# One convolution-attention and expert kernel: the norm's power ahead of the diagonals, table rows filled in the first stage, and steps of the convolution and of the experts moved between stages

## The chip, the cores and the metric

The kernel runs on one core of a Trainium2 chip. The metric is the device time of one execution in microseconds (us), as a median over runs. Engines are named as the profile names them: PE (TensorE, matrix products), PEld (its weight loads, which run beside the products), DVE (VectorE), ACT (ScalarE), POOL (GpSimd) and SP (SyncE, which here only issues transfers). ACT and POOL issue transfers too. Each engine runs its own list of instructions in order.

## The reference, cut to what matters

```python
def _gn(v, G=32, eps=1e-5):           # group norm over channels and places
    ...
    return ((g - m) / jnp.sqrt(s + eps)).reshape(v.shape)

# layer 0; x is (2, 256, 56, 56), f32
def _L0_conv_ref(x, w_qkv1, w_qkv2, rpb0, rpb1, w_proj):
    y = jnp.einsum('oc,bchw->bohw', w_qkv1, x)              # 256 -> 768 channels
    y = jax.lax.conv_general_dilated(y, w_qkv2, (1, 1), 'SAME', feature_group_count=3 * C)
    ...                                                     # q, k, v of 8 heads
    outs.append(_natten2d(q[:, sl], k[:, sl], v[:, sl], rpbs[s], 7, DILATIONS[s]))  # 7x7, dilation 1 and 2
    ...
    return jnp.einsum('oc,bchw->bohw', w_proj, o)
x = x + _L0_conv_ref(_gn(x), ...)

# layer 1; tokens t, 3136 for each of two images
    Q = jax.nn.elu(q) + 1.0
    K = jax.nn.elu(k) + 1.0
    KV = jnp.einsum('nshd,nshv->nhdv', K, v)                # sums over all tokens of an image
    msg = jnp.einsum('nlhd,nhdv,nlh->nlhv', Q, KV, Z) * L
    msg = _layernorm(msg.reshape(N, L, C) @ Wm, g1, b1)
    h = jax.nn.relu(jnp.concatenate([x, msg], axis=-1) @ W1) @ W2
t = t + (x + _layernorm(h, g2, b2))
    ...
    probs = jax.nn.softmax(xt @ Wr + br, axis=-1)           # 8 experts, the best 2 for each token
    h = jax.nn.gelu(jnp.einsum('end,edh->enh', xe, W1) + b1[:, None, :], approximate=False)
    y = jnp.einsum('enh,ehd->end', h, W2)
t = t + (weights[:, :, None] * sel).sum(axis=1)
```

## The kernel before, in words

**Stages.** The two images are shifted against each other, so that work of two kinds is there at any time.

1. Start and first stage (0 to 418 us): image 0 is loaded and normed, its convolution runs, and then image 0's neighbourhood attention runs while image 1 is normed and part of its convolution is made. At the end the projection of image 0 is added to the input and written as tokens to `td`.
2. Key sums of half 0, image 0's tokens (460 to 547 us): for each tile of tokens a layer norm, keys and values, and their sums.
3. Groups of half 0 (547 to 780 us): queries, message, feed-forward, router and the scatter of routed tokens into the rows of `xs`.
4. The seam (780 to 860 us) and attention of image 1 (to 1078 us), between whose steps stand the first steps of the experts.
5. Key sums of half 1 (1106 to 1211 us), its groups (1211 to 1476 us) and the router's tail (1476 to 1511 us), with further experts' steps.
6. The last stage (from 1511 us): all other expert tiles, one after the other, and the output.

**Norm and convolution** (class `Convolutions`, L400). An image lies in `x_sb` as two blocks of 128 channels by 3136 places. `load_x` fetches it in two halves of columns, block 0 on SP's queue and block 1 on ACT's. `norm_image` takes statistics in seven columns of G = 448 places (bn_stats on DVE), sums them over a group by a small matrix product, and `rstd_of` takes the power -1/2 on POOL; then DVE norms `x_sb` in place, in two halves. It is a generator: image 1's runs between taps of image 0's last block. `run` makes a qkv block (`oc`, six of them, in two halves `hf`): four products of eight rows into `py` (L510), each copied by ACT into the padded `ypad` (L516), and then nine taps into `yc`. While `share` is in force (the first stage), eight rows of a half go to PE: nine diagonal matrices `diag` are made by POOL (L500) and multiplied (L529), and DVE does the other rows. Without it (the rest of image 1's convolution, run inside layer 1) DVE does all the taps (L549), at a priority lowered by LATE. A store on SP (L564) closes a half of a block. What is left of it in layer 1 are 26 calls of the generator: 24 blocks `py`, one call ahead without PE work, and the last taps.

**Attention** (class `Attention`, L593). Bias tables are loaded by row as `tab0` and `tab1` in the pool `t`, one buffer each; the chunk's scores (L622), bias, Exp, sums and values follow. `residual` (L879) loads the input of two tiles into `x_s` on SP, ordered behind the newest convolution store `anchors["store"]`; `projection` takes it. The pools' letters give the order in which their memory is laid out: t tables, k keys, b bias, p probabilities, v values, r, x and ac for output and sums, l loads.

**Layer 1** (`linear`, L1574, called from `layer1`, L2059). It yields steps: `keys` 39 of them, then `steps` (L2041) takes a list of strings, `parts`, one for each group of tiles plus the drain. Each letter asks one generator for one step:

- q queries, m message, f feed-forward, r and p the router's two ends, P a scatter, w the merging of the sums, x preparation of the router
- k a step of the convolution (half 0 only)
- e a step of the experts (half 1 only); c has no work of its own

In half 0, `fill()` gives the convolution a step at every third step of the key sums. After `parts[7]` a loop empties the generator. Then come `ln.keep()`, the fill of `y2` (L2093, a tile with constants) and seven fills of `xs` (L2096, 256 rows of 260 floats each, the rows that pad short expert lists), and the load of the first experts.

**Experts** (class `Experts`, L1283). Tiles have 256 routed rows. `ex.run` yields two steps ahead and eight per tile; a step is eight products (L1536 into `ph`, or L1554 into `py`), and a finished tile is added to `y2` by an indirect transfer on POOL (L166). NFI = 13 tiles run early: as steps inside attention of image 1 from its step LEAD = 12 on, inside the key sums of half 1 and at the letters e. The other NFS - NFI = 35 full tiles and NHS = 5 half tiles run in the last stage.

**What sets the order.** On PE, layer 1 and attention of image 1 run exactly as written (`tc.manual_schedule`). On the other engines, and on PE in the first stage, a planner orders the instructions: it simulates when operands are there, and prefers what comes earlier in the code, unless `tc.high_priority` shifts it (a negative offset puts it last). `tc.issue_after(ins)` keeps an instruction behind `ins` if both are on the same engine; on another engine it orders nothing:

```python
with tc.issue_after(anchors["store"]):
    ld = nc.sync.dma_start(x_s[:, :, : kn * TT], xv[b, :, :, i * TT : (i + kn) * TT])
```

`anchors["pow"]` is the newest power of a norm (on POOL), `anchors["store"]` the newest store of the convolution (on SP). `rstd_of` is a helper; its lines L149 and L259 appear in the profile.

## Time and profile before

| what | number |
|---|---|
| median of 3 runs | 2087.62 us |
| lowest, highest | 2083.85, 2088.35 us |
| profiled execution, its own time | 2087.87 us |
| its span | 2086.1 us |
| instructions | 27767 |
| bytes moved by DMA, mean rate | 268.78 MB, 129 GB/s |
| L510 on PE (`py`, qkv blocks) | 384, 152.4 us |
| L1536 and L1554 on PE (experts) | 1440 and 1360, 306.9 and 303.7 us |
| L166 on POOL (indirect transfers of experts) | 101, 162.3 us |
| L529 on PE (diagonals) | 324, 132.6 us |

The page of the profile gives for each engine the busy time and its share of the span, the number of instructions behind an x, and the chain of work that ended last. A view by stretch gives the same busy times for a window of the span. A waits' line names the engine that waited, what it then ran, "<-" and the instruction that released it, and behind the colon the total in us, the number of waits and the longest one. In a line of the timeline the first two numbers are start and duration, and a number in square brackets is the time from which the operands were there, with what came last. "SPq" is SP's queue of transfers. PE's clock is the granted clock as a share of full speed. The longest groups of instructions are those of the table; all PE groups together make the 89% busy share.

### The profile page before, as it was taken

How to read it: one execution, taken by the hardware profiler on the slowest of the kernel's cores; microseconds unless marked ns; L12 is line 12 of the kernel's file. 1: busy time of each engine (PE TensorE's matmuls, PEld its weight loads, DVE VectorE, ACT ScalarE, POOL GpSimd, SP SyncE). 2: the span in 40 equal slices, each digit the busy share in tenths (PEclk: the TensorE clock that was granted, in tenths of full speed). 3: DMA queues.
4: the chain of work that ended last, by engine and by line, in shares of the span. 5: the costliest groups of instructions: out<-in, count | busy, mean ns of one | idle time of the engine just before them, and what ended most of it. 6: DMA issues, size and time to landing. Idle time of an engine off the chain costs nothing.

```text
span 2086.1 us, 27767 instructions
## 1 busy us (share of the span) xinstructions
PE 1857.6 (89%) x9996; PEld 1320.8 (63%) x9996; DVE 1071.3 (51%) x2696; ACT 678.2 (33%) x1271; POOL 630.4 (30%) x738
## 2 busy tenths in 40 slices
PE   4999998967889994799988899999599999999996
PEld 2545454545646553566666665567488888888885
DVE  4988988858977654465554333555342111211121
ACT  1333333312334322444433433334122222222332
POOL 4532110037211444111115611234433333333231
PEclk9999899989999996799999999999799999999998
DMA  5542431250101228664475121011387766766895
GB/s 119 138 120 81 135 110 44 79 172 16 39 31 39 69 89 235 146 158 125 113 204 155 49 58 38 31 51 54 97 241 209 201 192 190 199 194 190 281 286 173
DMA packets 198426, 268.78 MB, mean 129 GB/s; under 512 B 30377, under 2 KB 157399, under 8 KB 198033
## 3 DMA queue, kind: packets, MB, share of 16 engines
q1 hardware_dynamic: 173584, 230.43, 36.1%
q0 software_dynamic: 19728, 27.54, 7.2%
q10 hardware_dynamic: 4960, 8.88, 1.2%
q8 instruction: 83, 1.36, 0.3%
q14 instruction: 71, 0.57, 0.1%
HBM read 200.11 MB, written 70.95 MB: 130 GB/s over the span
## 4 chain that ended last, share of the span: by engine, by line
PE 69%; DVE 12%; DMA 7%; POOL 5%; ACT 3%; issue 3%; SPq 0%; ACTq 0%; DVEq 0%; POOLq 0%
PE ph L1536 13%; PE py L1554 12%; PE p L1849 8%; PE pc L529 4%; PE py L510 4%; PE po L636 4%; PE py L1865 4%; PE x L1554 2%; DVE yc L549 2%; PE x L1536 2%; DMA y<-yt,idi 2%; PE pm L1819 2%; PE s_ps L622 2%; DVE yc L556 2%; PE pq L1779 2%
## 5 line engine op out<-in xcount | busy, mean ns | idle before, releaser
L1536 PE MATMUL ph<-xe,w1e 128*128 128x256 f32 (+1 forms) x1440 | 306.9, 370 | 4.0 <-ACT hT L1540 2.2
L1554 PE MATMUL py<-w2e,hT 128*128 128x256 f32 x1360 | 303.7, 380 | 0.0
L1540 ACT ACTIVATE hT<-ph,sv 128x256 f32<-128x256 f32 (+1 forms) x360 | 165.1, 461 | 406.9 <-PE ph L1536 396.5
L1536 PEld LDWEIGHTS ph<-xe,w1e 128*128 128x128 f32 x1440 | 262.8, 191 | 39.4 <-ACT hT L1540 2.5
L1554 PEld LDWEIGHTS py<-w2e,hT 128*128 128x128 f32 x1360 | 255.0, 191 | 33.7 <-issue 1.7
L166 POOL DMA_INDIRECT y<-yt,idi x101 | 162.3, 1607 | 270.3 <-DVE yt L1560 126.7
L556 DVE SCALAR_TENSOR_TENSOR yc<-ypad,w,yc 128x1120 f32<-128x1120 f32 x144 | 199.3, 1385 | 27.9 <-ACT yc L546 25.3
L510 PE MATMUL py<-x_sb,wq 128*128 128x448 f32 (+1 forms) x384 | 152.4, 531 | 12.9 <-DVE x_sb L481 9.6
L259 POOL TENSOR_TENSOR rs<-rs,mhalf 128x2 f32<-128x2 f32 (+3 forms) x90 | 69.2, 773 | 312.3 <-DVE rs L258 231.2
L627 DVE TENSOR_TENSOR p<-p,tab 112x952 f32<-112x952 f32 (+5 forms) x88 | 122.1, 1391 | 61.8 <-ACT p L626 56.3
L626 ACT ACTIVATE p<-s_ps 112x952 f32<-112x952 f32 (+5 forms) x88 | 102.1, 1160 | 138.1 <-PE s_ps L622 92.7
L529 PE MATMUL pc<-ypad,diag 128*128 128x448 f32 x324 | 132.6, 549 | 0.0
L1492 DVE CAST idi<-xr 128x2 int32<-128x2 f32 (+1 forms) x53 | 10.9, 205 | 235.3 <-DMA xr<-xs 235.3
L1560 DVE SCALAR_TENSOR_TENSOR yt<-py,eq,yt 128x256 f32<-128x256 f32 x85 | 41.0, 483 | 164.7 <-PE py L1554 164.7
L1518 POOL TENSOR_SCALAR yt<-b2e,eq 128x256 f32<-128x256 f32 x101 | 48.8, 490 | 242.5 <-DMA b2e<-in_L_ffn_b 180.4
L510 PEld LDWEIGHTS py<-x_sb,wq 128*128 128x128 f32 x384 | 72.2, 197 | 75.5 <-issue 55.8
L166 POOL DMA_INDIRECT xs<-row,si x98 | 96.5, 984 | 70.9 <-DVE si L1985 37.0
L549 DVE SCALAR_TENSOR_TENSOR yc<-ypad,w,yc 128x784 f32<-128x784 f32 x96 | 109.0, 1145 | 7.3 <-ACT yc L546 6.2
L636 PE MATMUL po<-p,v 98*32 98x170 f32 (+5 forms) x960 | 69.9, 370 | 32.9 <-DVE p L627 15.8
L1849 PE MATMUL p<-m2T,fw 128*128 128x512 f32 (+2 forms) x224 | 95.2, 549 | 0.0
L305 PE MATMUL kx<-xt,ks 128*128 128x256 f32 (+1 forms) x200 | 59.1, 446 | 39.7 <-DVE ks L242 39.7
L1849 PE MATMUL p<-xT,fw 128*128 128x512 f32 (+1 forms) x208 | 94.0, 576 | 0.0
(370 smaller groups left out, 2927.0 us busy)
## 6 DMA issues: line engine op xcount, KB each, us to landing
w1e<-in_L_ffn_W SPq DMA_DIRECT2D x53, 1024.0 KB
w2e<-in_L_ffn_W SPq DMA_DIRECT2D x53, 1024.0 KB
yd<-yc SPq DMA_DIRECT2D x24, 784.0 KB
ld<-yd SPq DMA_DIRECT2D x28, 448.0 KB
xr<-xs SPq DMA_DIRECT2D x48, 260.0 KB
b2e<-in_L_ffn_b SPq DMA_DIRECT2D x53, 128.0 KB
t<-td SPq DMA_DIRECT2D x12, 512.0 KB
y<-t SPq DMA_DIRECT2D x24, 256.0 KB
```

Of the source, the lines that this page charges most:

```text
L166: ins = nc.gpsimd.indirect_dma_start(out=dst[:, :], out_offset=bass.IndirectOffsetOnAxis(ap=index, axis=0), in_=src, in_offset=None, **kw,)
L510: nc.tensor.matmul(py[:, :n, :], self.wq1[:, ct, oc * P : (oc + 1) * P], self.x_sb[:, ct, (q0 + g0) * WW : (q0 + g0 + n) * WW], start=(ct ...
L529: nc.tensor.matmul(pc, diag[:, tap, :], ypad[:, dy : dy + SHARE, dx : dx + WW], start=(tap == 0), stop=(tap == 8),)
L549: nc.vector.scalar_tensor_tensor(yc[:, y0:y1, :], src, w, yc[:, y0:y1, :], ALU.mult, ALU.add)
L556: nc.vector.scalar_tensor_tensor(yc[:, y0:y1, :], src, w, yc[:, y0:y1, :], ALU.mult, ALU.add)
L626: nc.scalar.activation(p[:nk, :, :n], s_ps[:nk, :, :n], AF.Exp)
L627: nc.vector.tensor_tensor(grid(p), grid(p), table[:nk], ALU.mult)
L636: nc.tensor.matmul(dst[hs] if w is None else den[hs], v[:nk, hs] if w is None else w[:nk, :], p[:, h, :, o : o + q.shape[2]], start=first ...
L1536: nc.tensor.matmul(p1, x.w1[:, ct, j * P : (j + 1) * P], x.xe[:, ct, :], start=(ct == 0), stop=(ct == 1),)
L1540: nc.scalar.activation(hT[:, j, :], p1, AF.Gelu, bias=x.sv[:, 4 + j : 5 + j])
L1554: nc.tensor.matmul(py, hT[:, j, h * P : (h + 1) * P], x.w2[:, j, :], start=(j == 0), stop=(j == NJ - 1),)
L1849: nc.tensor.matmul(p1[:, :w], fw1[:, k, oc * P : (oc + 1) * P], rhs, start=(k == 0), stop=(k == 3))
```

## The change

It has five parts.

1. **Norm.** `load_x` fetches an image in four pieces of columns (448, 896, 896, 896) instead of two. The power stands under `tc.high_priority()`. The norm is applied in three pieces (448, 1120, 1568 columns) instead of two. The diagonals stand on POOL behind the newest power.
2. **First stage.** The projection at the end of image 0 keeps two residual loads ahead, in three buffers instead of two, and from strip 3 on they are not ordered behind a store. The pools of image 0's attention and of `linear` for half 0 are laid out in another order. For image 1, `tab0` has two buffers.
3. **Fills.** The fill of `y2` and the seven of `xs` stand ahead of layer 1 in the code, under `issue_after(anchors["pow"])`, instead of behind its first eight parts.
4. **Convolution in half 0.** The key sums give it a step at i = 0, 1, 2, 13, 19, 25, 31 and 37 (8 instead of 13), the parts 16 instead of 13: two more strings have a third k and a second, so the k per string are 4, 3, 3, 2, 2, 2 instead of 4, 3, 3, 2, 1, 0. The last two calls are left to the loop after part 7.
5. **Experts.** NFI is 14: one tile more runs early. The key sums of half 1 give 23 steps instead of 15. In the strings of half 1 the letters e move from the middle parts, 6 to 8, towards their ends and to the last parts; some of the other letters there change their order.

```diff
-NFI = 13
+NFI = 14
...
         def load_x(self, b):
-            for hf in range(2):
-                cols = slice(hf * T // 2, (hf + 1) * T // 2)
+            for c0, c1 in zip((0, G, 3 * G, 5 * G), (G, 3 * G, 5 * G, T)):
+                cols = slice(c0, c1)
                 for ct in range(2):
...
-            grs, anchors["pow"] = rstd_of(sp, gps[:, 2:4], 1e-5, "gn")
-            yield
-            for hf in range(2):
-                cols = slice(hf * T // 2, (hf + 1) * T // 2)
+            with tc.high_priority():
+                grs, anchors["pow"] = rstd_of(sp, gps[:, 2:4], 1e-5, "gn")
+            yield
+            for c0, c1 in zip((0, G, T // 2), (G, T // 2, T)):
+                cols = slice(c0, c1)
...
-                        for tap in range(9):
-                            nc.gpsimd.tensor_scalar(
-                                diag[:, tap, :], ident, w2[:, oc, tap : tap + 1], 1.0, ALU.mult, ALU.mult
-                            )
+                        with tc.issue_after(anchors["pow"]):
+                            for tap in range(9):
+                                nc.gpsimd.tensor_scalar(
+                                    diag[:, tap, :], ident, w2[:, oc, tap : tap + 1], 1.0, ALU.mult, ALU.mult
+                                )
...
-                t = self.pool["t"].tile([TT, NH * (KR[s] + 6) * nw], F32, name=f"tab{s}")
+                t = self.pool["t"].tile(
+                    [TT, NH * (KR[s] + 6) * nw], F32, name=f"tab{s}", bufs=2 if self.banks and s == 0 else 1
+                )
...
-                x_s = xp.tile([P, 2, 2 * TT], F32, name="x_s")
+                x_s = xp.tile([P, 2, 2 * TT], F32, name="x_s", bufs=2 if banks else 3)
                 i = e[j] + k0
-                with tc.issue_after(anchors["store"]):
+                with tc.issue_after(anchors["store"]) if banks or j < 3 else nullcontext():
...
-                        acc, items = strip(j)
-                        for _, k0, kn in items:
-                            projection(acc, j, k0, kn, residual(j, k0, kn))
+                        items = [(j, k0, min(2, e[j + 1] - e[j] - k0)) for k0 in range(0, e[j + 1] - e[j], 2)]
+                        loaded = deque(residual(*item) for item in items[:2])
+                        acc, _ = strip(j)
+                        for k, item in enumerate(items):
+                            projection(acc, *item, loaded.popleft())
+                            if k + 2 < len(items):
+                                loaded.append(residual(*items[k + 2]))
                             yield 0
...
-        att = Attention(ctx, 0, "l t k b p v r x ac")
+        att = Attention(ctx, 0, "l k b t p v r x ac")
...
-        pools = {k: pool(f"p3{k}", bufs[k]) for k in ("q e t w k l s", "e s t q k w l")[half].split()}
+        pools = {k: pool(f"p3{k}", bufs[k]) for k in ("e t q w k l s", "e s t q k w l")[half].split()}
...
+        with tc.issue_after(anchors["pow"]) if behind else nullcontext():
+            nc.sync.dma_start(y2[N : N + ST, :], a["c_fill"][0, :, 0:C])
+            for i in range(NDUM):
+                rows_i = slice(E * RG + i * ST, E * RG + (i + 1) * ST)
+                nc.sync.dma_start(xs[rows_i, :], a["c_fill"][E + i])
         with ExitStack() as ph:
             ln = linear(ph, tk, 0, behind)
             with tc.manual_schedule(engines={mybir.EngineType.PE}):
                 for i, _ in enumerate(ln.keys()):
                     if i == 5:
                         ln.feed()
-                    if i % 3 == 1:
+                    if i < 3 or (i > 8 and i % 6 == 1):
                         fill()
...
-                    "mqfkfPPPPmkqfrfrff", "mqfkpPPPPfmqfrfrff", "mqfpPPPPfmqfrfrff",
+                    "mqfkfPPPPmkqfrfrff", "mqfkpPPPPfmkqfrfrff", "mqfkpPPPPfmkqfrfrff",
...
             ln.keep()
-            nc.sync.dma_start(y2[N : N + ST, :], a["c_fill"][0, :, 0:C])
-            for i in range(NDUM):
-                rows_i = slice(E * RG + i * ST, E * RG + (i + 1) * ST)
-                nc.sync.dma_start(xs[rows_i, :], a["c_fill"][E + i])
...
-                    if i < 3 or i % 3 == 1:
+                    if i < 3 or i % 3 == 1 or (i < 27 and i % 3 == 2):
                         next(tiles, None)
...
-                    "qewexewexqwexqq", "meqemeq", "meqefmqfefefff",
+                    "qewexewexqwexqq", "meqemeq", "meqfmqfeffff",
...
-                    "mqfpcfmfqrfPPfPrPfe", "mqfpfmfqePePrePfePref", "mfefpefmeferePPfePerPe",
-                    "fefeepefeferePfePere", "eeeeperPePer", "eeeepP",
+                    "mqfpcfmfqrfPPfPrPf", "mqfpfmfqPPrPfPref", "mffpfmfrePPfPerPe",
+                    "ffepfefreePfePere", "eepeereePeePer", "eeepePe",
```

## The prediction

> **What bounds the kernel now.** I read the page first (engine shares, the chain), then busy time by stretch, then the waits inside each stretch with idle TensorE, then the order of the instructions there. The page says TensorE is the bound: 1857.6 us busy of 2086.1, and the chain is 69% PE. So the work itself stays, and only the 228 us without it can go. This view by stretch (length, then busy us of PE, PEld, DVE, ACT, POOL, then PE clock, DMA share, GB/s) shows where they lie:
>
> ```profile
> PE 1857.6 (89%) x9996; PEld 1320.8 (63%) x9996; DVE 1071.3 (51%) x2696; ACT 678.2 (33%) x1271; POOL 630.4 (30%) x738
> ...
> 0.00:36.00 36.00, 6.69 (x13) 3.39 (x13) 13.13 (x29) 2.03 (x4) 10.09 (x35) 0.99 0.54 137
> 418.00:460.00 42.00, 24.18 (x89) 17.32 (x90) 22.87 (x78) 3.57 (x6) 14.32 (x24) 0.76 0.69 213
> 460.00:547.00 87.00, 70.11 (x292) 52.52 (x291) 76.02 (x119) 28.40 (x48) 58.79 (x53) 0.94 0.05 19
> 620.00:780.00 160.00, 157.36 (x603) 96.06 (x601) 97.70 (x395) 53.31 (x146) 55.20 (x62) 1.00 0.18 59
> 780.00:860.00 80.00, 42.14 (x276) 25.48 (x277) 33.76 (x153) 19.64 (x33) 25.84 (x33) 0.59 0.76 197
> 1106.00:1211.00 105.00, 85.57 (x401) 70.89 (x399) 41.56 (x132) 44.92 (x64) 63.45 (x84) 0.97 0.28 81
> 1476.00:1511.00 35.00, 13.99 (x71) 11.62 (x70) 15.37 (x112) 3.90 (x11) 16.30 (x17) 0.69 0.40 118
> 1511.00:1958.00 447.00, 445.60 (x2120) 392.52 (x2120) 101.11 (x363) 117.42 (x248) 140.58 (x157) 0.99 0.71 202
> ```
>
> The idle places are the start (29 us), the end of image 0 and the first key sums (18 + 17), the seam into image 1 (38), the second key sums (19) and the router's tail (21). From 620 to 780 and from 1511 on TensorE is full; there any work added costs its price. Next the waits of PE in 418 to 547, in 1106 to 1211 and in the tail, and one of SP before the seam (total us, times, longest), then the start in order of time:
>
> ```profile
> PE kx L305 <- DVE ks L242: 23.7, 12, 6.8
> ...
> PE kx L305 <- DVE ks L242: 16.0, 11, 3.7
> ...
> PE pp L1976 <- DVE chosen L1968: 20.6, 3, 9.2
> ...
> SPq L2096 <- DMA xs<-row,si: 16.0, 1, 16.0
> ```
>
> ```profile
> 18.43 6.26 POOL L500 TENSOR_SCALAR diag<-ident,w 128x128 f32<-128x128 f32 x18 [15.95 <-DMA w<-in_L_conv_w_qkv]
> ...
> 25.45 0.72 POOL L149 TENSOR_TENSOR rs_gn<-rs_gn,mhalf 128x2 f32<-128x2 f32 x1
> ...
> 35.25 0.23 ACT L370 ACTIVATE pf<-pf 84x33 f32<-84x33 f32 x1 [31.02 <-DMA pf<-frame]
> ...
> 35.95 5.22 PE L510 MATMUL py<-x_sb,wq 128*128 128x448 f32 x8 [3.12 <-ACT ypad L516]
> ```
>
> **A, the start.** The input of the power is there at 17.96 and the power runs at 25.45, behind 18 diagonals. Moved ahead: 7.5 us earlier. The first norm piece shrinks from 1568 to 448 columns, from 1.03 us (four took 4.12) to about 0.3: 0.7 more. But the gain meets a second wait. ScalarE's queue holds `pf`'s Exp (L370) ahead of the first `ypad` copies, and that Exp waits for a DMA until 35.25; TensorE had two banks full at 32.8 and stood 3.1 us for it. If ScalarE's order stays, TensorE resumes at 35.95 as before: gain 0. If all copies of the first block come ahead of the Exp, two banks are full at 27.36 - 8.2 + 5.5 = 24.6, and the gain is 11.3. The second Exp, at 39.01, stands in the same queue. The order is the planner's, and its times shift by only a few us, so some copies pass and not all: I take -4.5. x in four pieces per row block instead of two puts four more issues of about 0.43 us on the two queues (1.7 us, half on SP ahead of `frame`), so the Exp may come 1 us later. Statistics: the last wave holds 4 of 14 bn_stats instead of 8, 4 x 0.54 = 2.1 us at best; I count it in the -4.5. Upper end: the seven fills below get ahead of the second `pf` load on SP, 1.9 MB at the 231 GB/s of the stretch from 780 to 800 is 8 us: +8.
>
> Against cutting x speaks the Trainium skill, "DMA: Bandwidth & Descriptors", "Anatomy of one DMA": about 2.0 us fixed for each DMA, bytes on top. The row: the second halves (1.61 MB on both queues) were ready at 10.94, 3.8 us after the first at 7.17, which is 426 GB/s with no fixed cost between. By the page, if two more waves each paid it, A would be -0.5; by the row it stays.
>
> The same edit applies to image 1. Its diagonals now queue behind its power at 249.94; they were made at 237.07 in 4.13 us, and their first use is at 266.42, so 250.7 + 4.1, or 11.3 (the longest nine diagonals took), ends before that: free, but without that cover up to 7 us. Two more norm operations on DVE: 0.1 us; the first matmul starts about 0.7 earlier. **B** is this and the end of image 0: residual loads two ahead in three buffers, and from strip 3 not behind a store. The last residual went out at 428.63, `w_k` and the token loads stand behind it on SP, tokens land at 436.14 and PE waits 6.8 us for their norm. With a buffer more it can go after the third item's transposes, about 426.4: -2. The projections themselves wait for the one `s_ps` tile, which stays. The pools' new order lets tokens land where `l` and `k` lay; these are done by 403, as the tables are by 407: nothing before the residual. B together -2.5, from -6 to +2.
>
> **C, key sums to groups.** The convolution has 24 blocks left (L510), about 1.25 us of PE each, and 96 taps (L549) of 1.14 us on DVE, 16 to a chunk of four blocks. Calls needed: 26. Before, 13 in the key sums and 13 in the groups. After, 8 (three at once at the start, where PE waits 6.8 us anyhow) and 16; the last two fall to the loop that empties the generator, after part 7, at the seam. In 460 to 547 the taps are 53.5 of DVE's 76.0 us; one chunk (18.3) is left of them. PE has 70.1 - 7 x 1.25 = 61.4 us there, and of 17 us idle, which wait for `ks` behind taps, I keep 8: 87 - 70 = -17. Given back: five blocks go into a stretch that is full, 5 x 1.25 = +6.3, and 18 us of taps among DVE's 97.7 of 160 cost about 1 us of lateness. C -10; ends: -20 if idle goes altogether and the moved blocks find gaps, +5 if ks stays late for POOL's sake (58.8 of 87 us busy).
>
> **D, the seam, 780 to 860.** Removed: seven fills (1.9 MB, 4.44 us of SP at 776.18, after 16.0 us in which SP stood for scatters). Their bytes sit in front of the loads that end PE's waits: `ld` took 9.28 us to land, `tab` 6.32. Without 8 us of traffic `ld` lands some 5 us sooner. The p of the first chunk, 7.5 us late, has a second cause: `sv` before it on DVE waits for POOL's scatters to 812.7; half gained, say 0 to 7. Two buffers for the first table let its second row load ahead of `w1e` and `w2e`; the wait until 850.32 (6.3 us, table landing) goes. The 8.7 us for `ld` behind 4 MB of weights stays, and is late next. Added: block 24 (1 us PE), 16 taps (18.3 us, DVE has 46 free but queues in order), and eight Experts loads (4 us of SP) that waited for x_sb at 648 and now wait until 779, in front of the tables; the late tap of 1.1 us on some of the router's steps: +4. D = -5 - 3 - 6 + 4 = -10; ends -20 and, with the store below, +15.
>
> Clock: granted 0.59 in that stretch. The skill's "TensorE: Matmul & The Clock Gate", Part 1, says an idle window of about 3.4 us halves it; by that rule, shorter waits would also speed part of the 42.1 busy us, and D could reach -18. I left it out of the sum.
>
> The fills land in the first 100 us instead, DMA share 0.51 there from 36 on; SP issues them in its gaps (4.44 us). The next need of that queue, attention's `ld` at 71.8, feeds PE at about 100: hidden; uncovered, the 8 us of A's upper end.
>
> **E, experts.** Steps of `tiles`: 2 + 8 per tile, 106 before, 114 now. Attention takes 65 in both. Before: 15 in the key sums, 26 in parts 0 to 8; the 21 after that find nothing. Now: 23 in the key sums, 10 in parts 0 to 2, none to part 6, 1, 3, 7, and 5 of 9 in part 10. A step is eight matmuls, 1.75 us. The eight new ones in the key sums stand just where PE waits for `ks` (16.0 us in 11): cost 6 instead of 14, -8. In the tail, twelve steps (21 us) stand among three waits of 7.5, 9.2 and 3.9; by position one step precedes the first, three the second, none the third, and the rest lengthens the chain: they cover about 10. Given back: parts 6 to 8 lose ten steps, waits of 1.8 to 3.6 us such as those at 1421 to 1425 appear: +3; a tile's POOL work (two scatters of 1.6, so 0.4, two yt of 0.49, 4.6 us) stands in the router's queue: +3. E = -12. One tile, 14.25 us from one `ph` to the next, leaves the full last stage and appears here: no sum of its own. Ends -20 and +3.
>
> **Sum** against the profiled execution, 2087.87 us (span 2086.1 and 1.8 around it; median 2087.62): -4.5 - 2.5 - 10 - 10 - 12 = -39: 2049, said as 2050.
>
> **Rivals.** (1) All lower ends: 2088 - 77 = 2011, some of it won't add, 2020; for it: every wait named has another engine idle; against: `sv` and `pf`. (2) Given back: A 0 behind `pf`, C -3 since 620 to 780 is full, D -3, E -5, B -2: 2075. (3) Slower: SP's order puts the last convolution store (L564) ahead of the seam's loads. It must wait for 16 taps that start after 778. In the profile two such stores held SP 78.3 us, the longest 48.2, harmlessly, as nothing was due. At the seam attention's loads are. Held to about 812 (778 + 18.3 + DVE's own 12.7 + copies) it costs 27 and the sum is near zero; 48 gives 2088 - 39 + 10 + 48 = 2107. It decides from 33 us on. Against it: DVE is less than half busy there and the planner ranks taps last. (4) The fills change nothing because SP already floated the y2 fill to 33.55; but the xs fills did stand at 776.
>
> **How the numbers follow.** Likeliest 0.45, its own range 2032 to 2068; given back (2068 to 2083) 0.20; all (under 2032) 0.13; no change 0.05; slower 0.17. Faster 0.78, same 0.05 (within 0.2%, 4.2 us, about what a measurement of this kernel tells from none), slower 0.17. The range 2020 to 2094 leaves out about 0.06 below and 0.13 above.
>
> **What would show it.** Power before the diagonals near 18, and PE's first steady run well before 36, with `pf`'s Exp behind some `ypad` copies (A). First key sums about 17 us shorter, L510 in them seven (C). No xs fill from 776 to 781, PE busy above half from 780 on (D). Waits of `kx` for `ks` in the second key sums halved, experts in the tail, 34 full tiles in the last stage (E). Wrong would be: SP standing in L564 at the seam, a router tail 10 us longer than what its steps take, or the last stage not 14 us shorter.

## The result, and the profile after

The changed kernel took 2102.37 us (median of 3, 2101.07 to 2105.39) against 2087.62: a ratio of 1.0078, interval 1.0053 to 1.0104. It is slower, by 15 us, where 2050 had been forecast. The profiled execution spans 2099.0 us, 12.9 more than that of before.

First the same stretches as before, in the view by stretch (length, then busy us of PE, PEld, DVE, ACT, POOL, then PE clock, DMA share, GB/s), behind the page's line of the engines:

```profile
PE 1868.1 (89%) x9996; PEld 1324.4 (63%) x9996; DVE 1067.6 (51%) x2700; ACT 677.8 (32%) x1271; POOL 636.1 (30%) x738
...
0.00:36.00 36.00, 10.28 (x21) 5.67 (x22) 13.71 (x31) 2.90 (x5) 13.09 (x38) 0.92 0.53 140
418.00:460.00 42.00, 26.25 (x91) 17.46 (x92) 24.98 (x76) 5.59 (x9) 13.61 (x25) 0.80 0.67 208
460.00:547.00 87.00, 65.75 (x271) 50.46 (x270) 54.19 (x108) 20.54 (x37) 51.23 (x55) 0.88 0.02 10
620.00:780.00 160.00, 160.00 (x615) 98.08 (x613) 104.50 (x397) 55.90 (x149) 59.62 (x61) 1.00 0.17 57
780.00:860.00 80.00, 39.03 (x253) 23.57 (x252) 39.34 (x166) 19.12 (x35) 28.07 (x33) 0.59 0.73 188
1106.00:1211.00 105.00, 92.17 (x430) 77.87 (x428) 43.61 (x136) 43.79 (x65) 65.35 (x85) 0.95 0.36 101
1476.00:1511.00 35.00, 26.85 (x132) 22.24 (x130) 12.21 (x69) 10.26 (x21) 15.90 (x17) 0.90 0.32 91
1511.00:1958.00 447.00, 433.64 (x2039) 379.31 (x2040) 106.88 (x412) 116.00 (x241) 140.93 (x156) 0.98 0.68 192
```

Two rows answer the prediction at once. From 460 to 547 DVE lost 22 of its 76.0 us (the prediction's taps come to 35), and PE did not get denser: 65.8 busy instead of 70.1, at a granted clock of 0.88 instead of 0.94, and the stage ends where it ended. From 1511 on PE, full before (445.6 of 447), is no longer: 433.6.

Fixed windows slide when a stage is longer, so the rest is read from landmarks of PE: the first or last product into a tile that only one stage uses. The landmarks of a single profile move by several us, in the first stage above all (the first key product of half 0 lies between 435.4 and 444.9 in fifteen profiles with the new start), so lengths of stages are compared, and means where there are several. The profiles are before and after and those of the runs below.

| stage, from landmark to landmark | old form, us | new form, us | difference |
|---|---|---|---|
| start to first key product `kp` (5 and 15 profiles, means) | 440.1 | 441.6 | +1.5 |
| first `kp` to last `pk`, key sums half 0 | 104.1, 104.2 | 99.7 to 102.7, 7 profiles, mean 101.2 | -2.9 |
| last `pk` to last `p`, groups half 0 | 224.3, 222.9 | 225.2 to 226.0, 7 profiles | +2.3 |
| last `p` to first `po` of image 1, seam | 42.2 to 45.0, 5 profiles, mean 43.6 | 46.4 to 46.7, 11 profiles | +3.0 |
| key sums half 1, with 15 and with 23 expert steps | 103.1, 103.2 (101.0 to 106.0 in 6 profiles) | 113.6 to 115.4, 5 profiles, mean 114.6 | +11.4 |
| last `pk` to last `pp` of half 1, groups and tail | 299.5 (299.2 to 302.4 in 6 profiles) | 304.9 (298.9 to 304.9 in 3 profiles) | +5.4 |
| last `pp` to last `ph`, last stage | 547.1 | 540.0 (540.0 to 543.6 in 3 profiles) | -7.1 |

What the prediction had as -39 us is thus +13: A and B +1.5, C -0.6, D +3.0 (and in the attention behind it +0.8 in the mean, with a scatter of 5 us), E +9.7. The +1.5 and the +5.4 are inside the scatter of their landmarks, the other rows are not. Groups, tail and last stage together are steadier: 846.6 to 850.6 us with the old strings and 13 tiles, 842.5 to 844.9 with the new ones and 14, so the tile that was to take 14.25 us off them took 2 to 8. PE's waits in the first key sums (460 to 547), then in the second (1106 to 1226), then in the tail and the head of the last stage (1476 to 1620):

```profile
PE kx L305 <- DVE ks L242: 21.3, 11, 6.3
...
PE ph L1544 <- ACT hT L1548: 7.0, 5, 2.3
PE kx L305 <- DVE ks L242: 5.3, 4, 1.6
PE pts L275 <- DVE xe L1520: 2.4, 2, 1.2
...
PE pp L1984 <- DVE chosen L1976: 9.6, 2, 5.5
PE ph L1544 <- ACT hT L1548: 6.5, 2, 5.4
PE ph L1544 <- DVE xe L1520: 3.3, 2, 2.2
PE px L1517 <- DMA xr<-xs: 1.8, 1, 1.8
```

Every wait that the experts' steps took away in the second half has an heir: for `ks` 16.0 us became 5.3, but the steps themselves now wait for `hT` and `xe`; in the tail a wait for `hT` of 5.4 us is new; in the last stage, where PE had waited 1.1 us, it waits 5.1 us for an expert tile's rows and what is made of them.

### The profile page after: what moved, and what is told of

Read it like the earlier page. It is cut to its first block, busy times and chain, and to the rows that moved or that the text cites. A ratio compares the mean times of both kernels' runs of the same rounds, so it can differ in the third digit from the quotient of the medians.

```text
span 2099.0 us, 27775 instructions
## 1 busy us (share of the span) xinstructions
PE 1868.1 (89%) x9996; PEld 1324.4 (63%) x9996; DVE 1067.6 (51%) x2700; ACT 677.8 (32%) x1271; POOL 636.1 (30%) x738
## 4 chain that ended last, share of the span: by engine, by line
PE 68%; DVE 11%; DMA 8%; ACT 4%; POOL 4%; issue 4%; SPq 1%; another core or an unknown queue 0%; ACTq 0%; DVEq 0%; POOLq 0%
PE py L1562 12%; PE ph L1544 12%; PE p L1857 7%; PE py L512 5%; PE pc L531 5%; PE po L638 4%; PE py L1873 3%; PE x L1562 3%; PE kx L305 2%; PE x L1544 2%; DVE yc L551 2%; DMA y<-yt,idi 2%; PE s_ps L624 2%; PE pm L1827 2%; PE pq L1787 2%
## 5 line engine op out<-in xcount | busy, mean ns | idle before, releaser
L1544 PE MATMUL ph<-xe,w1e 128*128 128x256 f32 (+1 forms) x1440 | 315.4, 376 | 17.2 <-ACT hT L1548 13.5
L1544 PEld LDWEIGHTS ph<-xe,w1e 128*128 128x128 f32 x1440 | 266.0, 194 | 55.7 <-ACT hT L1548 15.3
L259 POOL TENSOR_TENSOR rs<-rs,mhalf 128x2 f32<-128x2 f32 (+3 forms) x90 | 68.6, 766 | 267.9 <-DVE rs L258 237.9
L1500 DVE CAST idi<-xr 128x2 int32<-128x2 f32 (+1 forms) x53 | 11.4, 215 | 239.9 <-DMA xr<-xs 239.9
L166 POOL DMA_INDIRECT xs<-row,si x98 | 103.3, 1054 | 83.0 <-DVE si L1993 46.0
L551 DVE SCALAR_TENSOR_TENSOR yc<-ypad,w,yc 128x784 f32<-128x784 f32 x96 | 100.7, 1061 | 2.9 <-ACT yc L548 2.1
L531 PEld LDWEIGHTS pc<-ypad,diag 128*128 128x128 f32 x324 | 60.8, 193 | 53.3 <-issue 49.4
```

The lines of the kernel that those rows point to most:

```text
L166: ins = nc.gpsimd.indirect_dma_start(out=dst[:, :], out_offset=bass.IndirectOffsetOnAxis(ap=index, axis=0), in_=src, in_offset=None, **kw,)
L531: nc.tensor.matmul(pc, diag[:, tap, :], ypad[:, dy : dy + SHARE, dx : dx + WW], start=(tap == 0), stop=(tap == 8),)
L551: nc.vector.scalar_tensor_tensor(yc[:, y0:y1, :], src, w, yc[:, y0:y1, :], ALU.mult, ALU.add)
L1544: nc.tensor.matmul(p1, x.w1[:, ct, j * P : (j + 1) * P], x.xe[:, ct, :], start=(ct == 0), stop=(ct == 1),)
```

## The experiments

Ratios are to the kernel before, run beside, with a 95% interval. Three questions came in this order: which part lost the time, why the key sums did not get shorter, what the seam and the last stage wait for.

### Which part lost it

**The experts' part undone.**

```diff
-NFI = 14
+NFI = 13
-                    if i < 3 or i % 3 == 1 or (i < 27 and i % 3 == 2):
+                    if i < 3 or i % 3 == 1:
...
-                    "ffepfefreePfePere", "eepeereePeePer", "eeepePe",
+                    "fefeepefeferePfePere", "eeeeperPePer", "eeeepP",
```

> The changed kernel with the experts' part undone (13 early tiles, 15 steps in the second key sums, the letters e as before). Theory: the experts' part is what made the kernel slower, about 10 of the 13 us between the two spans, since its steps lengthen the router's tail; this run is then at about 2092 us (2088 to 2096). Rival: the loss was there before the experts (start, key sums, seam), and this run stays at 2100 to 2104.

2089.02 us, ratio 0.9997 (0.9981 to 1.0013): no change from before. The theory holds, with two consequences. E costs 13 us by these medians (14 when each is set against its own kernel before), 10 by its stages; and the other four parts together, forecast at -27, are worth nothing.

**The experts' part alone**, on the kernel before (the same edit the other way).

> The kernel before with the experts' part alone. Theory: about 2098 us, 10 more than before, with the second key sums some 10 us longer for 14 us of steps, and the tail from the last full group to the first tile of the last stage some 17 us longer. Rival (the experts' part only loses together with the other parts, which delay it): 2086 to 2090.

2095.46 us, 1.0035 (1.0017 to 1.0052), which is 7 us slower, a little less than expected. The second key sums took 115.4 us instead of 103.1, groups and tail 303.2 instead of 299.5, the last stage 541.5 instead of 547.1. So it loses alone, and the interval leaves it open whether it loses more in company.

**The letters as before, with the tile and the 23 steps kept.**

```diff
-                    "mqfpcfmfqrfPPfPrPf", "mqfpfmfqPPrPfPref", "mffpfmfrePPfPerPe",
-                    "ffepfefreePfePere", "eepeereePeePer", "eeepePe",
+                    "mqfpcfmfqrfPPfPrPfe", "mqfpfmfqePePrePfePref", "mfefpefmeferePPfePerPe",
+                    "fefeepefeferePfePere", "eeeeperPePer", "eeeepP",
```

> The changed kernel with 14 early tiles and 23 steps in the second key sums, but the letters e of the strings as before (26 steps, none left for the last three strings). Theory: the place of the steps in the tail costs the time, not the tile: the tail is then as short as before (33 us from 1478 to 1511), the last stage a tile shorter but for 4 to 7 us of waits, and the whole 2092 to 2095 us. Rival (the tile costs more early than late, wherever it stands): 2100 to 2104.

2095.15 us, 1.0031 (1.0014 to 1.0047). Groups and tail are back at 300.9 us, 4 less than with the new letters; as other profiles of the new letters lie between 298.9 and 304.9, the stage alone does not show it, and what carries the reading are the medians, 2095.15 and 2102.37. The last stage stayed at 542.1, so the tile brings 5 us there, not 14.25.

**The new strings, with 13 tiles.**

```diff
-NFI = 14
+NFI = 13
```

> The changed kernel with 13 early tiles: the strings stay, and the eight steps that are missing leave the last strings empty. Theory: the tail loses eight steps of 1.75 us that lengthened the router's chain and the last stage gains a tile of 14.25 us without its waits; 2090 to 2095 us. Rival (tail and last stage exchange the tile one for one): 2100 to 2104.

2094.68 us, 1.0020 (1.0005 to 1.0035). Eight steps fewer make groups and tail 289.2 us instead of 304.9, 15.7 for 14 us of products: in the sum these steps were not covered at all. They did fill waits (for `chosen` PE waits 18.6 us here and 9.6 with them), but other waits came in their place. The last stage went from 540.0 to 547.5. A tile that costs its full price early saves half of it late.

What the tail's steps do is in ACT's timeline of the changed kernel there (start, length, instruction, and in brackets the idle time before and what ended it):

```profile
1506.46 0.47 ACT L1548 ACTIVATE hT<-ph,sv 128x256 f32<-128x256 f32 x1 [0.39 <-PE ph L1544]
1507.73 0.47 ACT L1548 ACTIVATE hT<-ph,sv 128x256 f32<-128x256 f32 x1 [0.79 <-PE ph L1544]
1508.22 1.28 ACT L1909 ACT_TABLE_LOAD   x1
1512.79 0.22 ACT L1909 ACTIVATE prob<-prob 128x16 f32<-128x16 f32 x1 [3.29 <-DVE prob L1908]
1513.02 1.28 ACT L1548 ACT_TABLE_LOAD   x1
1514.32 0.84 ACT L1548 ACTIVATE hT<-ph,sv 128x256 f32<-128x256 f32 x2
```

```profile
1511.16 0.41 DVE L153 TENSOR_SCALAR row<-t_ab,mv,rs 128x256 f32<-128x256 f32 x1 [3.28 <-DMA xs<-row,si]
```

The experts' Gelu and the router's Exp take turns on ACT, in order. The Exp holds the queue 3.3 us until DVE has its input, and DVE for its part waits 3.28 us for the landing of a scatter (the second view, of DVE). Each change of function loads a table for 1.28 us. Together that is PE's 5.4 us for `hT`. From the last feed-forward product to the end of the router there are four such loads (5.1 us), before there was one. The prediction had looked at PE's gaps in the tail and counted them as cover, not at the queue that the steps need besides PE.

### Why the key sums stayed as long

**No convolution step in the key sums of half 0.**

```diff
-                    if i < 3 or (i > 8 and i % 6 == 1):
+                    if False:
                         fill()
```

> The changed kernel without the experts' part and without any step of the convolution in the key sums of half 0; all eight go to the loop behind part 7, so that the seam is longer and only the key sums are looked at. They take 101 us from the first key product to the last, with eight steps, and 104 in the kernel before with 13. Prediction's theory (the taps on DVE make the sums late): 80 to 88 us. Rival (a chain of its own from one tile to the next sets the pace: key product, two steps of ACT, DVE, sum product, norm of the next tile): 95 to 101 us.

102.9 us. No step at all is no shorter than eight. It is a single run, 2114.73 us in all, as the steps now stand at the seam. The view of this stage, 442 to 544, for this kernel:

```profile
442.00:544.00 102.00, 69.40 (x269) 54.87 (x268) 36.55 (x113) 17.45 (x32) 52.16 (x69) 0.80 0.08 24
```

No engine is full: DVE has 36.6 us of 102, and PE waits 32.6 for `ks`. So taking the steps out does not shorten this stage. It does not show that taps are free: with the taps go blocks of PE, and the granted clock from the first `kp` to the last `pk` falls, 0.89 with thirteen steps, 0.87 with eight, 0.80 with none. DVE's wait of the norm (`xt`) for PE's sum product `kx`, in the kernel before, without the experts' part and without any step, grows with it:

```profile
DVE xt L153 <- PE kx L305: 2.3, 1, 2.3
...
DVE xt L153 <- PE kx L305: 12.8, 6, 3.5
...
DVE xt L153 <- PE kx L305: 26.8, 9, 3.9
```

In the chain of work through this stage the taps have 23.8% with thirteen steps, 13.4% with eight and nothing with none, and `kx` 9.6, 22.8 and 31.9%: one path gave way to another of about the same length. How much of that is the clock no run isolated. What both paths share is seen in POOL's timeline, here of the changed kernel without the experts' part:

```profile
475.17 1.26 POOL L288 TENSOR_TENSOR t<-t,b 128x512 f32<-128x512 f32 x1
476.39 0.70 POOL L259 TENSOR_TENSOR rs<-rs,mhalf 128x2 f32<-128x2 f32 x1
477.17 0.20 POOL L261 TENSOR_TENSOR up_t<-rs 128x2 f32<-128x2 f32 x1
478.59 1.26 POOL L312 TENSOR_TENSOR kacc<-kacc,ks 128x512 f32<-128x512 f32 x1 [1.23 <-DVE ks L242]
482.57 1.18 POOL L285 TENSOR_SCALAR t<-t,up 128x256 f32<-128x256 f32 x2 [2.71 <-DVE xt L153]
483.83 1.27 POOL L288 TENSOR_TENSOR t<-t,b 128x512 f32<-128x512 f32 x1
485.06 0.70 POOL L259 TENSOR_TENSOR rs<-rs,mhalf 128x2 f32<-128x2 f32 x1
```

The power of the next tile's norm (L259) stands on POOL behind the update of this tile (L285) and the addition of b2 (L288), while DVE waits for that power (L282, 15.3 us in this stage) and POOL for DVE (18.5 us). It is a loop, and it closes through PE: norm on DVE, update, addition and power on POOL, `up` and `ks` on DVE, `kx` on PE, and the next norm on DVE, which waits for `kx`. All three engines are idle part of the time.

**The addition of b2 left out** (the b2 of these inputs is zero; the kernel no longer computes the addition).

```diff
-        nc.gpsimd.tensor_tensor(t, t, b2[p].unsqueeze(1).to_broadcast([rows, n, C]), ALU.add)
```

> The changed kernel without the experts' part, leaving out the addition of b2 to the tokens in the key sums (25 POOL operations of 1.27 us or half as long in each half, whose operand is zero in these inputs). Theory A: POOL's queue, with the power of the norm in it, paces the key sums; they fall from 101 to 92 to 97 us in half 0 and from 103 to 95 to 99 in half 1. Theory B: the chain runs through ACT and DVE and POOL is beside it: 100 to 101 and 102 to 103.

The key sums fall from 101.0 to 92.0 us and from 103.2 to 93.5, theory A. It is a single run, 2070.54 us. DVE's wait for the power, without the experts' part and here:

```profile
DVE up L282 <- POOL rs L259: 15.3, 9, 2.5
...
DVE up L282 <- POOL rs L259: 6.3, 8, 1.2
```

**The addition moved to the queries of the same tokens**, for 512 tokens at a time.

```diff
         def queries(n0, n, out):
...
+            t = tk.at(n0, n)
+            nc.gpsimd.tensor_tensor(t, t, b2.unsqueeze(1).to_broadcast([P, n, C]), ALU.add)
```

> The changed kernel without the experts' part, with the addition of b2 moved from the key sums to the queries of the same tokens (13 POOL operations of about 2.5 us in the groups, where POOL is busy 55 of 160 us). Theory: POOL's queue paces the key sums, so both fall as in the run that left the addition out (101 to 92, 103 to 94 us) and nothing is lost in the groups: 2069 to 2076 us. Rival (POOL's additions delay the router's powers and scatters in the groups): key sums as short, groups 8 us or more longer, 2080 to 2088.

2097.94 us, 1.0055 (1.0031 to 1.0079): a miss of both. The key sums took 102.8 us, and POOL's groups in them show why:

```profile
L1783 POOL TENSOR_TENSOR t<-t,b 128x1024 f32<-128x1024 f32 x6 | 14.1, 2348 | 0.5
```

All six additions of half 0 ran inside the key sums: the tokens are ready there, and the planner takes what is ready. Moved in the code, they did not move in the queue.

**The same on the kernel before.**

> The kernel before with the same move of the b2 addition: 13 steps of the convolution in the key sums, not 8. Theory: once POOL is off, DVE (85.6 of 103 us busy there with 13 steps, 65.5 with 8) comes next, and the convolution's part is worth what the prediction said of it at most here: key sums of half 0 96 to 100 us against 92, the whole 2072 to 2080. Rival (the steps are covered in either case): 92 to 93 us and the same time as the run beside it.

2088.55 us, 1.0001 (0.9986 to 1.0015), key sums 105.7 us, for the same reason. It says nothing of DVE.

**Held: the moved addition ordered behind the last sum on POOL.**

```diff
+            with tc.issue_after(anchors["summed"]):
+                nc.gpsimd.tensor_tensor(t, t, b2.unsqueeze(1).to_broadcast([P, n, C]), ALU.add)
```

`anchors["summed"]` is the newest L312.

> The changed kernel without the experts' part, with the b2 addition in the queries and there ordered behind the last addition of the key sums on POOL, so that it cannot come back into them. Theory (POOL's queue paces the key sums): 101 to 92 us in half 0, 103 to 94 in half 1, and nothing lost in the groups, where the six additions (14 us) stand in front of the first power that is due some 25 us later: 2070 to 2076 us. Rival (the groups lose what the sums gain, since the first message waits for that power): groups 8 us or more longer, 2084 to 2090.

2087.74 us, 1.0016 (1.0000 to 1.0031). The key sums are 94.0 and 97.0 us, but from the last `pk` to the first `p` of half 0 it is 61.7 us instead of 53.9, and groups and tail of half 1 take 306.7 instead of 299.5, so the gain goes back, as the rival had it.

**Held, on the kernel before.**

> The kernel before with the same held additions: 13 steps of the convolution in the first key sums instead of 8. Theory (POOL off, DVE is next, so that the steps now count): key sums of half 0 96 to 100 us, 4 to 8 more than beside it, the groups 2 to 4 us less, the whole 2072 to 2078. Rival (the steps are covered in either case): 92 to 94, and the time of the run beside it within 2 us.

2076.25 us, 0.9957 (0.9940 to 0.9974). This is faster than both kernels. With all 13 steps of the convolution the key sums take 91.4 us, no more than with eight (94.0): the rival's side. Its stage, 438 to 529:

```profile
438.00:529.00 91.00, 75.05 (x318) 56.73 (x319) 82.36 (x157) 29.62 (x50) 54.01 (x58) 0.95 0.16 50
```

Here DVE is at 82 of 91 us, and the granted clock is 0.95 (0.86 from 439 to 533 in the run with eight steps): the steps that were to leave cost nothing here.

**Held, on the whole change.**

> The whole changed kernel with the same held additions. Theory: the second key sums take 23 expert steps of 1.75 us each with PE as the bound (85.6 us of products with 15 steps, 99.6 with 23), so they fall only from 114 to 103 to 108 us, and the whole to 2084 to 2090, still above the run without the experts' part by 8 to 14. Rival (POOL was what made the experts' steps dear there): second key sums below 103 us and the whole within 4 us of the run without them.

2090.42 us, 1.0025 (1.0008 to 1.0042). The second key sums took 104.7 us against 97.0 with 15 steps, 7.7 for 14 us of products: PE, busy 93.7 of the 104.7 us at full clock, bounds them now, as expected. In the total E costs 2.7 us by the medians, less than the 8 to 14 expected; on that the rival was right.

**Spread: the addition at the end of each message, behind that message's power** (`issue_after(newest[1])`, the newest power), on the kernel before, on the change without experts and on the whole change.

> The kernel before with the b2 addition at the end of each message, ordered on POOL behind the power of that message (one of 2.35 us for each group, not six in a block). Theory: the key sums keep their 91 to 93 us of half 0 and 94 to 97 of half 1, and the groups get back the 8 and 4 us that the block cost: 2064 to 2070 us. Rival (the first groups are late for the same reason as before, the merge of the sums on DVE): groups as long as with the block, 2074 to 2078.

> The changed kernel without the experts' part, with the same spread additions. Theory: the four other parts bring nothing and cost 2 to 4 us at the seam and 2 to 4 in the groups; 2069 to 2077 us, 4 to 9 more than the run beside it. Rival (they are worth something once the key sums are short): at most the time of the run beside it.

> The whole changed kernel with the same spread additions. Theory: the experts' part costs 4 to 10 us here too, by the second key sums (103 to 106 us against 94 to 97) and the tail: 2076 to 2085 us. Rival (with the sums short its steps are covered): the time of the run without it.

2079.34 us, 0.9964 (0.9943 to 0.9985); 2090.04, 1.0011 (0.9995 to 1.0027); 2092.80, 1.0036 (1.0015 to 1.0057). Spreading gave back some of the first groups (65.0 to 59.9 us up to the first `p`) and took most of it from the later ones (168.0 to 171.8), so it is no better than the block; its theory's 2064 to 2070 was missed. But the three stand in a row: without the change fastest, with its first four parts 11 us more, with all of it 13 to 14. The same row of the held ones is 2076, 2088, 2090. Once the key sums are short the four parts cost about 11 us. By two pairs of profiles 2 to 3 us of that is the start (inside its scatter), 3 to 4 the seam, 2 to 3 the key sums and 1 to 2 the groups; the rest lies in stages that the four parts do not touch and is not explained.

### The seam and the last stage

The changed kernel's SP queue at the seam, and PE's waits there (from the last `p` to the first `po`) in three kernels without the experts' part: as it is, with the fills back, with no late convolution.

```profile
783.60 0.46 SPq L1305 DMA_DIRECT2D sel<-in_ln_g_t  x1
...
787.20 0.43 SPq L1316 DMA_DIRECT2D cumA<-in_c_cum  x1
787.74 1.01 SPq L763 DMA_DIRECT2D ld<-yd  x2
...
801.29 0.35 SPq L566 DMA_DIRECT2D yd<-yc  x1
801.74 0.44 SPq L763 DMA_DIRECT2D ld<-yd  x1
```

```profile
PE po L638 <- DVE p L629: 8.2, 1, 8.2
PE x L731 <- DMA ld<-yd: 5.0, 3, 2.1
PE pc L1331 <- DVE cnt L1981: 4.7, 1, 4.7
```

```profile
PE x L731 <- DMA ld<-yd: 11.3, 3, 9.9
PE po L638 <- DVE p L629: 6.9, 1, 6.9
PE pc L1331 <- DVE cnt L1981: 4.9, 1, 4.9
```

```profile
PE po L638 <- DVE p L629: 10.3, 1, 10.3
PE x L731 <- issue: 2.2, 1, 2.2
PE x L731 <- DVE qT L748: 2.0, 1, 2.0
```

**Fills back.** (`ln.keep()`, and behind it the fill of `y2` and the seven of `xs`, as before.)

> The changed kernel without the experts' part, with the fills behind the first parts again, as in the kernel before. From the last feed-forward product of half 0 to the first value product of image 1 the kernel before takes 43.8 us, the changed one 46.6. Theory: moving the fills did free the queue and the traffic, and the convolution's late steps (eight loads and a store in front of attention's loads) cost more than that; with the fills back both are there, and the stretch is 50 to 53 us, the whole 4 to 6 us above 2089. Rival: the fills cost nothing where they were, since attention's loads wait for other things; 46 to 48 us and no change.

55.8 us in the seam, 2102.99 in all, 1.0065 (1.0039 to 1.0092). The fills in front of `ld` cost 9.2 us, if the eight loads and the store stand there too. The whole is 14 us above the run without the experts' part, where 4 to 6 were expected; what it lost beyond the seam is not explained.

**No late convolution step.**

```diff
-                    if i < 3 or (i > 8 and i % 6 == 1):
+                    if i < 3 or (i > 8 and i % 6 == 1) or i in (16, 28):
```

> The changed kernel without the experts' part, with two more steps of the convolution in the key sums (10 instead of 8), so that none is left for the loop behind part 7. Theory: the eight loads of the experts' constants and the store leave the seam, which is then 40 to 43 us instead of 46.6, and the key sums grow by 1 to 2 us only; the whole about 2085 us. Rival: the seam waits for the scatters and the router whatever the queue holds; 46 us, and 2089.

44.7 us, 2088.22 in all, 1.0015 (0.9993 to 1.0037): the rival, nearly. The key sums took 103.3 us, 2.3 more. The four cases of the seam are: fills and no late steps (before) 43.6; late steps and no fills (the change) 46.6; both 55.8; neither 44.7. Each alone costs 2 us at most, and taking the fills away could only gain back what the change itself had put there. What stays is `po` waiting for `p`, which grows as `ld` gets earlier, 8.2 to 10.3 us: DVE has `sv` in front of it, and `sv` waits 7.9 us for POOL (7.3 in the kernel without late steps), which is in twice eight scatters 1.26 us apart.

**`sv` of the first experts ordered behind the first p.**

```diff
+            early = self.tk.run == 0 and t < 2 and nh == 2
+            with tc.issue_after(anchors["first"]) if early else nullcontext():
+                nc.vector.tensor_reduce(x.sv, so, AX.X, ALU.add)
```

> The changed kernel without the experts' part, with the first two experts' constants (sv on DVE, which waits 7.9 us for POOL behind sixteen scatters) ordered behind attention's first p instead of in front of it. Theory: this order sets the end of the seam; from the last feed-forward product to the first value product 38 to 42 us instead of 46.6, the whole 2082 to 2085. Rival (the landing of ld comes next, in the same microsecond): 45 to 47 us and 2089.

The seam is 41.7 us, as expected, and the attention behind it 264.6 instead of 259.6 (257.2 to 262.9 in the other profiles of it): what was gained is gone by the end of the stage, and 2093.18 us, 1.0036 (1.0014 to 1.0059), is not better. Which wait took it over was not isolated.

**The last stage's tables and fills asked for earlier**, on the whole change.

```diff
-                    if i > 2:
-                        chunk(work)
+                    if i < 10:
+                        chunk(work)
+                    chunk(work)
```

> The whole changed kernel, but the tables and closing fills of the last stage are asked for two pieces a step from its first step on, instead of one from the fourth. Theory: with three early tiles instead of four at the head of that stage, its tables and fills end after the first late tile is due, which costs 4 us of waits, 1.8 of slower clock; asked for earlier they end in time: the stage falls from 540 to 533 to 536 us, the whole to 2095 to 2099 against 2102. Rival (the queue's own wait for the router's memory, 25.3 us, sets it): no change, 2100 to 2104.

2098.24 us, 1.0055 (1.0036 to 1.0074), the last stage 543.6, not 533 to 536: a miss of the stage. The whole lies in the expected range, but not for the stage's sake: in its profile groups and tail, which the edit does not touch, are 6 us shorter than in the changed kernel's, and the two intervals overlap (1.0053 to 1.0104 for the changed kernel). PE still waits 5.1 us for the first late tile's rows (`px <- DMA xr`). In the changed kernel SP stands long in front of all this:

```profile
SPq L1492 <- DVE sf L1992: 25.3, 1, 25.3
```

A load of the second tile of that stage waits for the router's last use of its memory, and the loads and eight closing fills behind it start only then. Before, four early tiles (57 us) covered fills and loads; three (43 us) do not. That the queue and not the chain of tables is to blame is read from these waits; no run took it apart.

## Why the prediction was wrong

- **A and B, -7: the mechanism was right, the gain did not last.** The power runs at 17.20, ahead of the diagonals, and PE starts at 18.52 instead of 27.36. As feared it stops behind `pf`'s Exp: 8.4 us, until ACT's copies at 33.4. The first diagonal products are 2.4 us earlier (means of 5 and 15 profiles, 38.0 and 35.6), the first transposes of attention 1.4, its first values 0.2, and the first key product is 1.5 later, which its scatter of several us does not tell from nothing. Of B, the last residual goes out at 427.98 instead of 428.63, while the first key product is 2 us later, and the wait that it was to shorten stays: PE waits 7.3 us for the first tiles' norm instead of 6.8. The mistake is the step from an earlier start to an earlier end: it never named what the first stage waits for, and no run isolated it. Cutting x in four did no harm to the statistics: they were in 0.9 us earlier (products of `gps` at 14.89 instead of 15.75). The Trainium skill's fixed cost of a transfer ("DMA: Bandwidth & Descriptors", "Anatomy of one DMA — SWDGE (gpsimd) path"), which in the prediction would have made A -0.5, did not show as a delay of them; that section is on transfers that GpSimd issues, and these go out on the queues of SP and ACT.
- **C, -10: wrong in its mechanism.** The failing step is "17 us of idle, which wait for `ks` behind taps, I keep 8". The profile's waits name what came last, `ks` on DVE; that it would come earlier without the taps was inferred from DVE's 76 busy us. Zero, eight, ten and thirteen steps give 102.9, 101.2, 103.3 and 104.1 us. A loop through POOL's queue holds them there (without the addition in it, 92.0), and fewer steps made PE's part of that loop slower, as the granted clock fell; the lower end of the range had it in half a sentence ("+5 if ks stays late for POOL's sake"). The price of the moved blocks was about right where it was paid: +4 to +5 of the forecast +6.3 between first and last `p`.
- **D, -10: right terms, wrong sum.** The eight loads (4.1 us) and the store were there, the store with 3.9 us of SP; the fills were gone, worth 9.2. The mistake was to take the fills' price (-5) from the order of before, where the run without late steps shows that `sv` and the scatters hide it. The second table's wait did not go either: 6.3 us again, and its loads (SP at 838.52) still stand behind `w1e` and `w2e` (821.93 and 822.49). The granted clock of the stretch stayed at 0.59, so what shorter waits might have added by a faster clock did not come either. The third rival, the store as the one thing that decides, needed 33 us of SP and got 3.9.
- **E, -12: wrong in sign.** Four terms were mis-sized. Steps "where PE waits for `ks`" were to cost 6 us of 14 and cost 11.4: PE's wait for `ks` fell by 10.7 us, but waits for `hT` and `xe` came (9.4 us, 3.4 before). With the addition held out of the loop they cost 7.7, so part of the price was POOL's queue; the rest was not taken apart. The tail's steps were to cover 10 us: from the last feed-forward product in front of the first of the three waits for `chosen` to the last `pp` it is 49.9 us instead of 32.6, so twelve steps (21 us) cost 17.3 and 3.7 were covered. The three waits did fall as forecast, from 20.6 to 9.6; what the prediction put at nothing is ACT's queue, where Gelu and Exp take turns, 6.5 us of waits for `hT`. Given back were to be 3 and 3; the groups in front of the tail, which the 21 us of steps had left, got only 11.9 us shorter and so gave back 9.1, a new wait for `chosen` of 6.0 among them (in the two other profiles of these strings 6.7 and 1.8 were given back). And "one tile, 14.25 us" that leaves the last stage was 7.1: 4 us of the missing 7 are PE's idle time, at the head of that stage, where the tile had covered loads and fills, and 3 are products that took longer.
- **Its own signs of being wrong.** A last stage not 14 us shorter came. A tail 10 us longer than what its steps take did not: it grew by 17 us for 21 us of steps. SP stood in the convolution's store at the seam for 3.9 us, not 33.
- **The chances.** Slower had 0.17, for the store alone. What made the kernel slower, steps that cost nearly their full price in the second key sums and a tile that gave back half of its own, had no rival; that steps lengthen the router's chain stood in the text with a cover of 10 and a +3. Four terms each took a gain from idle time without asking what keeps the idle time there.

## What to carry to other kernels

A wait's line names the last arrival, not the pacemaker. Before work is moved out of a stage or into its gaps, the loop from one tile to the next has to be followed through every queue, the half-idle ones too; taking one operation out of the suspect (here 16 us of POOL for 9 us of stage) tells it in one run. Where PE's work leaves a half-idle stage, the granted clock belongs beside the length: here it fell from 0.89 to 0.80. A moved piece of work also takes its cover along: ask what hid behind it where it stood. And where a planner orders an engine, moving a line moves nothing until an order holds it: look at the queue, not at the code.

## What the runs showed that was not expected

- One POOL operation put elsewhere gave what no part of the change gave: the addition of b2, held out of the key sums on the kernel before, makes it 2076.25 us (0.9957, 0.9940 to 0.9974), and left out, on the change without experts, 2070.54 in a single run.
- On ACT each change between Gelu and Exp cost a table load of 1.28 us: 56 in an execution, 15 of them (19.2 us) in the second key sums, with 15 expert steps and with 23 alike. The Trainium skill, "ScalarE: Activation LUTs", "What ACT_TABLE_LOAD costs", has 1283 ns for the load, which agrees, and a drain of about 1380 ns beside it; here the Gelu starts 0.02 us after the load's end (1513.02 + 1.28, 1514.32), and the load 0.01 us after the Exp's end (1512.79 + 0.22, 1513.02), so this switch has no room for a drain of that length.
- POOL's update of the tokens (L285) gets slower the more steps of the convolution run beside it: in mean 595 ns in the first key sums without steps, 877 with eight and 1091 with thirteen (about 550 when shortest). Taps on DVE and the rest of a step were not tested apart. It did not set the stage's length: without steps the updates are 6 us shorter in all than with eight, and the stage is no shorter.
- Profiles of kernels whose code is equal up to there differ by up to 9 us at the end of image 0 (435.4 and 444.4 in two of them), while the seam repeats within 0.3 us, the groups of half 0 within 1 and the key sums of half 0 within 3. The attention of image 1 (257.2 to 262.9) and the groups and tail of half 1 (298.9 to 304.9 with the same strings) scatter by 6. A change of a few us in the first stage or in these two is not to be read from one profile.
